# Seven 256-column products in place of four 512-column ones for the output projection of a state-space layer

## The chip, the core and the metric

The kernel runs on one core of a Trainium2 chip. A core has a matrix engine (TensorE, in the profile PE, with its weight loads as PEld), a vector engine (VectorE, DVE), a scalar engine (ScalarE, ACT), a general engine (GpSimd, POOL) and a queue engine (SyncE, SP) that issues most DMAs. Work is passed between them through SBUF and, for matmul results, through eight banks of PSUM. The metric is the device time of one launch in microseconds, over several runs.

## The reference

`reference()` computes a small model in float32 on x of 2 x 512 tokens x 512 features: a feed-forward layer, a state-space layer, the same feed-forward layer again, a memory layer, an attention layer, the memory layer again. The change is in the state-space layer (`_L0_attn_ref`): 128 heads of 64 channels make 8192 inner channels in 8 groups. The change touches what follows their gating:

```python
y = (Y_diag + Y_off).reshape(b, S, H_M, P_M)[:, :s] + D_res
y = y.reshape(b, s, D_INNER)
yg = y * jax.nn.silu(gate)
gsz = D_INNER // G_M
ygr = yg.reshape(b, s, G_M, gsz)
ygr = ygr * jax.lax.rsqrt(jnp.mean(ygr * ygr, axis=-1, keepdims=True) + EPS)
y = ygr.reshape(b, s, D_INNER) * gnorm_w
out = jnp.einsum('bsd,od->bso', y, out_proj_w)
return residual + out
```

Here b is 2, s 512, D_INNER 8192, G_M 8, and out has 512 columns. Because the norm is one factor per token and group, it can be applied after the product, group by group.

## The kernel before

The state-space layer is `ssm`. It goes through 128 steps, one for each of 64 tiles of 128 channels (`ct`) and each of two batches, in the order group g, batch b, tile q (eight tiles, so eight steps, for each group and batch; `PAIRS` is 8). `period(n)` writes out by hand the order of TensorE, VectorE, ScalarE and GpSimd for three steps in flight: `cur` (step n) is projected and convolved, `p1` (step n-1) has its state-space products, `p2` (step n-2) goes through the output projection. DMAs on SP aren't bound to that hand-written order; they are issued in the order that the scheduler of the framework chooses from it.

In a period TensorE goes through these lines:

- L1158, ht: four transposes of `p1.hid` (bank t). L1178 on VectorE multiplies them by dt into hc, L1187 on ScalarE by the decay into hd.
- L1128, called at many places: the seven products of two k-steps each that give hid and gate (already in Strassen's manner), into banks X, R and G, 256 columns at a time. ScalarE copies partial results between them (L1173 G, L1204 and L1242 u).
- L1213, st: states of `p1` from hd; VectorE chains them (L1223).
- L1078, po: the output projection, `gather`. For each of four chunks of 128 tokens one matmul: stationary a 128x128 piece of the gated result `yg`, moving the whole weight tile `wo` of 512 columns, summed into four banks `po` over the eight steps of a group. Chunks 0 and 1 come in the middle of the period, ahead of the last product into X ("ws3"), 2 and 3 at its end.
- L1268 and L1276, py: the state-space output of `p1`; VectorE adds the skip and multiplies with the gate (L1299, L1303 yg).

At the end of the period X is convolved: ScalarE L936 the first tap, VectorE L939 three more, ScalarE L1296 the silu, and the next period transposes it. `within` (L1047) and `times_c` (L1063) make the decay matrix M, ScalarE exponentiates it (L1055). GpSimd adds the squares of yg (L1123 ssum), makes Cs (L1068) from the broadcast `rows`, and in steps of batch 0 the sums of the next step's weights (L1024 to L1026, `add_up`), which `keep_sums` stores in DRAM for batch 1. In the sixth and seventh period of a group the next group's B and C are projected (L928), in the eighth their product (L986 cb) is made in bank t.

At a group's end `group_sums` and `group_norm` give the factor r, and `leave` (L1108) takes the four banks to x: four operations of 128x512, multiply and add, in the next period. The weight tile `wo` is loaded once for both batches (L348), scaled by `gnorm` on ScalarE (L1317) and kept in the pool `w2` of 12 tiles. After the 128 steps two more periods drain the pipeline, with the norm of the next feed-forward layer among them.

## Time and profile before

| | us |
|---|---|
| median of 3 runs | 2653.52 |
| lowest, highest | 2647.42, 2655.45 |
| the profiled execution | 2652.62 |
| its span, first to last instruction | 2650.9 |
| periods 1 to 127 of the state-space part (ht at 262.07 to ht at 2000.21) | 1738.1 |
| period 128 to the first matmul of the next layer (2018.92) | 18.7 |
| TensorE busy in L1078 (1024 passes) | 483.9 |

The page counts busy time per engine and follows one chain of waits back from the end. In its groups an f32 matmul appears as two records, one for each pass. The timeline merges neighbouring instructions of one line: start, time until the last of them ends, engine, line, operation, operands, shape, count, and in brackets how long the engine stood idle before and who released it. Matmuls overlap, so the step from one start to the next is what a group takes.

Period lengths repeat almost exactly from group to group: 13.31, 12.52, 12.52, 12.52, 15.96, 16.40, 13.60 and 12.55 us for the second to the eighth period of a group and the first of the next, the longer ones with L928, L986 and the group's sums. Periods 2 to 8, which also prepare decays for batch 1, take 105.8 us together.

### The profile page before, as it was taken

Reading aid. Unit: us, or ns where it says so; the run is one execution under the profiler, and the core shown is the slowest. Engines: PE = TensorE matmul, PEld = TensorE weight load, DVE = VectorE, ACT = ScalarE, POOL = GpSimd, SP = SyncE. Lnnn points to the kernel's source line nnn. Section 1 sums busy time; section 2 is a strip of 40 time slices with the busy share of each in tenths; the row PEclk is TensorE's granted clock in tenths of the full one; section 3 lists DMA queues with packets and bytes.
Section 4 is the critical chain, followed back from the end, with each engine's and each line's share of the span. In section 5 each row is a group of like instructions: output and inputs, shape, how many; then the busy total and the mean of one; then the engine's idle time right before and its main releaser. Section 6 shows DMA issues by size and latency. Waiting matters only on the chain.

```text
span 2650.9 us, 38083 instructions
## 1 busy us (share of the span) xinstructions
PE 2583.4 (97%) x13744; PEld 1685.5 (64%) x13744; DVE 1895.1 (71%) x4056; ACT 1587.9 (60%) x3247; POOL 597.0 (23%) x492
## 2 busy tenths in 40 slices
PE   8999999999999999999999999999998999899997
PEld 4445677777777777777777777777774444445453
DVE  7845987878778777777777878778786432666655
ACT  2214777777777677777777767777773211344433
POOL 0002322432332242242233234224320000111000
PEclk9999999999999999999999999999999999889988
DMA  6623444444444454444444444445441110000000
GB/s 204 197 78 116 175 151 168 181 150 189 156 175 167 153 192 153 166 171 175 175 159 165 179 162 171 171 153 192 152 175 42 40 59 24 1 1 2 1 1 32
DMA packets 90907, 342.93 MB, mean 129 GB/s; under 512 B 11520, under 2 KB 12096, under 8 KB 74208
## 3 DMA queue, kind: packets, MB, share of 16 engines
q1 hardware_dynamic: 87264, 330.86, 34.3%
q10 hardware_dynamic: 3168, 8.65, 0.8%
q8 instruction: 110, 1.80, 0.3%
q0 software_dynamic: 288, 0.98, 0.1%
q14 instruction: 77, 0.63, 0.1%
HBM read 295.10 MB, written 45.35 MB: 128 GB/s over the span
## 4 chain that ended last, share of the span: by engine, by line
PE 90%; DVE 6%; ACT 2%; issue 1%; POOL 0%; DMA 0%; SPq 0%; DVEq 0%; ACTq 0%; POOLq 0%
PE hid L1128 20%; PE po L1078 16%; PE gate L1128 9%; PE fmm L509 5%; PE fo L675 5%; PE py L1268 5%; PE st L1213 3%; PE py L1276 3%; PE fy L509 3%; PE cp_BT L928 2%; PE ht L1158 2%; PE cp_CT L928 2%; PE w L1806 1%; PE fdd L509 1%; PE pao L1866 1%; PE f L536 1%
## 5 line engine op out<-in xcount | busy, mean ns | idle before, releaser
L939 DVE SCALAR_TENSOR_TENSOR hid<-hid,small,hid 128x256 f32<-128x256 f32 (+3 forms) x768 | 368.7, 480 | 309.6 <-ACT hid L936 291.3
L1078 PE MATMUL po<-wo,yg 128*128 128x512 f32 x1024 | 483.9, 592 | 0.0
L1123 POOL TENSOR_TENSOR ssum<-ssum,sq 128x512 f32<-128x512 f32 x112 | 142.1, 1268 | 1048.8 <-ACT sq L1119 1048.8
L1047 DVE TENSOR_TENSOR_SCAN M<-rows,later 128x512 f32<-128x512 f32 x256 | 299.7, 1213 | 0.0
L1078 PEld LDWEIGHTS po<-wo,yg 128*128 128x128 f32 x1024 | 191.9, 190 | 127.7 <-issue 108.3
L1128 PE MATMUL hid<-mixed,wsum 128*128 128x256 f32 x1024 | 270.8, 387 | 0.3 <-ACT hid L1206 0.3
L1128 PE MATMUL hid<-hT_s,wgh 128*128 128x256 f32 x1024 | 264.7, 381 | 0.0
L1068 POOL TENSOR_TENSOR Cs<-CT,rows 128x768 f32<-128x768 f32 x128 | 233.4, 1823 | 2.0 <-PE hps_s L398 1.5
L1128 PEld LDWEIGHTS hid<-hT_s,wgh 128*128 128x128 f32 x1024 | 183.3, 190 | 23.0 <-ACT hid L1173 3.9
L1128 PEld LDWEIGHTS hid<-mixed,wsum 128*128 128x128 f32 x1024 | 184.0, 189 | 20.6 <-ACT hid L1206 0.7
L1187 ACT ACTIVATE hd<-ht,end 128x64 f32<-128x64 f32 x768 | 172.7, 330 | 9.1 <-DVE hc L1178 9.1
L1296 ACT ACT_TABLE_LOAD x128 | 164.2, 1283 | 2.3
L1063 DVE TENSOR_TENSOR M<-M,CB 128x512 f32<-128x512 f32 x256 | 164.4, 684 | 0.0
L1055 ACT ACT_TABLE_LOAD x127 | 162.9, 1283 | 2.2
L936 ACT ACTIVATE hid<-hid,small 128x256 f32<-128x256 f32 x256 | 143.6, 561 | 10.8 <-PE hid L1128 2.0
L1055 ACT ACTIVATE M<-M 128x512 f32<-128x512 f32 x256 | 147.8, 624 | 2.2 <-DVE M L1047 0.8
L1128 PE MATMUL gate<-mixed,wgh 128*128 128x256 f32 x512 | 141.6, 399 | 1.3 <-DVE v L1253 1.3
L1268 PE MATMUL py<-M,hc 128*64 128x128 f32 x2048 | 140.5, 280 | 0.0
L1128 PEld LDWEIGHTS hid<-hT_s,wsum 128*128 128x128 f32 x512 | 97.1, 190 | 67.9 <-issue 59.3
L1770 DVE CUSTOM_DVE_ANT_0 j<-s,future 128x384 f32<-128x384 f32 (+3 forms) x256 | 113.0, 487 | 37.2 <-PE s L1760 36.4
L1268 PEld LDWEIGHTS py<-M,hc 128*64 128x64 f32 x2048 | 109.6, 137 | 40.1 <-issue 37.7
L1128 PE MATMUL hid<-hT_s,wsum 128*128 128x256 f32 x512 | 131.5, 379 | 0.6 <-ACT u L1242 0.6
(341 smaller groups left out, 4606.0 us busy)
## 6 DMA issues: line engine op xcount, KB each, us to landing
rows<-rows SPq DMA_DIRECT2D x128, 1024.0 KB, 4.7
wgh<-in_w_gh_dram SPq DMA_DIRECT2D x128, 512.0 KB, 5.3
sums<-wsum SPq DMA_DIRECT2D x64, 512.0 KB, 3.0
wsum<-sums SPq DMA_DIRECT2D x64, 512.0 KB, 4.8
wo<-in_w_out_dram SPq DMA_DIRECT2D x64, 256.0 KB, 4.0
wbc<-in_w_bc_dram SPq DMA_DIRECT2D x16, 512.0 KB, 5.6
wi<-in_q_dram SPq DMA_DIRECT2D x44, 128.0 KB, 3.1
sc<-in_s_dram SPq DMA_DIRECT2D x44, 128.0 KB, 3.2
```

The costliest lines, as they stand in the source:

```text
L509: nc.tensor.matmul(dst, lhsT=w[:, k, :], rhs=x[:, k, :], start=start and k == 0, stop=stop and k == 1, skip_group_check=True,)
L936: self.nc.scalar.activation(out, p, AF.Identity, bias=w[:, 4:5], scale=w[:, 3:4])
L939: self.nc.vector.scalar_tensor_tensor(out=out, in0=p, scalar=self.convw[:, ct, 3 - s : 4 - s], in1=out, op0=ALU.mult, op1=ALU.add,)
L1047: self.nc.vector.tensor_tensor_scan(out=m, data0=cur.rows[:, i, 0, :], data1=self.later, initial=0.0, op0=ALU.add, op1=ALU.mult,)
L1055: self.nc.scalar.activation(m, m, AF.Exp)
L1063: self.nc.vector.tensor_tensor(out=m, in0=m, in1=sh["CB"], op=ALU.mult)
L1068: self.nc.gpsimd.tensor_tensor(out=cur.Cs, in0=sh["CT"][:, P:].unsqueeze(1).to_broadcast([P, 2, S - P]), in1=cur.rows[:, :, 1, P:], op=ALU ...
L1078: self.nc.tensor.matmul(self.po[c], lhsT=p2.yg[:, c * P : (c + 1) * P], rhs=self.wo[p2.ct], start=p2.q == 0, stop=p2.q == PAIRS - 1,)
L1128: self.nc.tensor.matmul(dst, lhsT=w[:, k, :], rhs=x[:, k, :], start=start and k == 0, stop=stop and k == 1, skip_group_check=True,)
L1187: nc.scalar.mul(hd[:, c, ch], pt[:, c, ch], self.dec["dt_end"][:, b1 * NC + c, h0 + i : h0 + i + 1],)
L1268: nc.tensor.matmul(py[ch, cs], lhsT=hc[:, c, ch], rhs=p1.M[i].rearrange("p (c t) -> p c t", c=NC)[:, c, :], start=c == 0, stop=c == 0, ski ...
L1296: nc.scalar.activation(cur.hid, cur.hid, AF.Silu)
```

## The change

- The output projection no longer runs step by step. The gated results `yg` of a group and batch are kept (eight tiles of two steps each, `pair_of`), and their projection runs during the next eight periods.
- For two neighbouring channel tiles, two chunks of tokens (h and 2+h) and the two halves of the output columns, the 2x2x2 block product is made with seven products instead of eight. A stage is one half h of a group and batch: seven products times four pairs of tiles, 28 matmuls of 256 moving columns, seven in each of four periods (`out_products`: four in the middle, one and two at the end). They go product by product, with three banks: OX, OR and OG; `out_seed` copies the first product from OX to OG.
- GpSimd makes the sums of yg that the products need (`out_sums`, 16 operations of 128x128 a stage).
- The weights are loaded two tiles at a time, scaled, their four differences made on GpSimd (`prepare`, `prepare_sums`), and all of it written to DRAM (`prepared`); each stage loads what it needs, 14 times 256 KB (`out_load`, a period ahead).
- `out_leave` adds a bank to a quarter of x: six operations of 128x256 a stage.
- hc, hd, st and the squares use buffers of other pools; `rows` is split in two loads, of which `starts` has one buffer and is read for Cs; `pr` has a bank of its own, and is no longer cleared by VectorE.
- `out_end` runs the last stages after the loop, with the first half of the next layer's norm between them; before, its statistics were in the last periods of the loop.

```diff
-            ctx.enter_context(self.banks("psum_s", t=1, po=4, X=1, G=1, R=1))
+            ctx.enter_context(self.banks("psum_s", t=1, OX=1, OG=1, OR=1, X=1, G=1, R=1, s=1))
             ctx.enter_context(self.in_order())
-            self.wo, self.done = {}, None
+            self.out_begin()
             self.load_rows(self.steps[0])
             for n in range(len(self.steps) + 2):
                 self.period(n)
+            self.out_end(len(self.steps) + 2)
...
     def load_rows(self, st):
-        st.rows = self.sp.tile([P, 2, 2, S], F32, tag="rows", name=f"rows{st.n}", bufs=2)
-        self.nc.sync.dma_start(
-            out=st.rows, in_=self.rows[st.b][st.h0 : st.h0 + 2].partition_broadcast(P)
-        )
+        rows = self.rows[st.b][st.h0 : st.h0 + 2].partition_broadcast(P)
+        st.rows = self.sp.tile([P, 2, S], F32, tag="rows", name=f"rows{st.n}", bufs=2)
+        self.nc.sync.dma_start(out=st.rows, in_=rows[:, :, 0])
+        st.starts = self.sp.tile([P, 2, S - P], F32, tag="starts", name=f"starts{st.n}", bufs=1)
+        self.nc.sync.dma_start(out=st.starts, in_=rows[:, :, 1, P:])
...
+    def out_begin(self):
+        self.pairs = [
+            self.sp.tile([P, 2, S], F32, tag=f"yg{i}", name=f"yg{i}", bufs=1)
+            for i in range(PAIRS // 2 + 1)
+        ]
+        self.A = {
+            x: self.sp.tile([P, PAIRS // 2, P], F32, tag=x, name=x, bufs=1)
+            for x in ("S1", "S2", "S34")
+        }
+        self.norms, self.banked, self.out_w, self.hold = {}, {}, {}, {}
+        self.made, self.raw = {}, None
+        half = lambda h: slice(h * HS, (h + 1) * HS)
+        low = lambda h: (0, slice(h * P, (h + 1) * P))
+        high = lambda h: (0, slice((2 + h) * P, (3 + h) * P))
+        odd = lambda f: lambda h: (1, f(h)[1])
+        self.order_out = [
+            ("OX", low, "raw", 0), ("OR", "S34", "sum", 2), ("OX", "S2", "sum", 1),
+            ("OG", odd(low), "raw", 2), ("OX", "S1", "sum", 0), ("OR", odd(high), "sum", 3),
+            ("OX", "S34", "raw", 3),
+        ]
...
+    def pair_of(self, i, k):
+        k = i % 2 * (PAIRS // 2) + k
+        if k <= PAIRS // 2:
+            return self.pairs[k]
+        name = "zeo"[k - PAIRS // 2 - 1]
+        if name not in self.hold:
+            self.hold[name] = self.early.tile([P, 2, S], F32, tag=name, name=f"yg_{name}")
+        return self.hold[name]
+    def prepare(self, n):
+        m, at = divmod(n, PAIRS)
+        g = (m + 1) // 2
+        if at % 2 == 0 or g == NG or m % 2 == 0 and m:
+            return
+        if at == 1:
+            self.made[g] = tuple(
+                self.dram.tile([PAIRS // 2, P, k, HS], F32, name=f"{x}{g}", tag=f"{x}{g}")
+                for x, k in (("oraw", 4), ("osum", 4))
+            )
+        ct = g * PAIRS + at - 1
+        self.raw = g, at // 2, [self.w2(self.a["w_out"][ct + k], f"wo{ct + k}") for k in range(2)]
+    def prepare_sums(self):
+        if self.raw is None:
+            return
+        g, i, raw = self.raw
+        for k in range(2):
+            ct = g * PAIRS + 2 * i + k
+            self.nc.scalar.mul(raw[k], raw[k], self.gnorm[:, ct : ct + 1])
+        made = [
+            self.w2pool.tile([P, 2, HS], F32, tag="w2", name=f"wos{g}_{i}_{k}") for k in range(2)
+        ]
+        (b11, b12), (b21, b22) = ((r[:, :HS], r[:, HS:]) for r in raw)
+        t1, t2, t3, t4 = (m[:, k] for m in made for k in range(2))
+        for out, in0, in1 in ((t1, b12, b11), (t2, b22, t1), (t3, b22, b12), (t4, b21, t2)):
+            self.nc.gpsimd.tensor_tensor(out=out, in0=in0, in1=in1, op=ALU.subtract)
+        self.raw += (made,)
+    def prepared(self):
+        if self.raw is None:
+            return
+        g, i, raw, made = self.raw
+        for dst, src in zip(self.made[g], (raw, made)):
+            for k in range(2):
+                self.nc.sync.dma_start(
+                    out=dst[i, :, 2 * k : 2 * k + 2],
+                    in_=src[k].rearrange("p (h d) -> p h d", h=2) if src is raw else src[k],
+                )
+        self.raw = None
...
+    def stage(self, n):
+        return divmod(n - PAIRS - 1, PAIRS // 2)
+    def out_load(self, n):
+        s, k = self.stage(n)
+        if not 0 <= s < 2 * NG * NB:
+            return
+        for one in range(7 * k, 7 * k + 7):
+            if one % 2 == 0:
+                bank, left, kind, part = self.order_out[one // 4]
+                raw, made = self.made[s // (2 * NB)]
+                ps = slice(one % 4, one % 4 + 2)
+                if kind == "raw":
+                    src = raw[ps, :, part]
+                else:
+                    src = made[ps, :, part]
+                t = self.w2pool.tile([P, 2, HS], F32, tag="w2", name=f"ow{s}_{one}")
+                self.nc.sync.dma_start(out=t, in_=src.rearrange("i p d -> p i d"))
+                self.out_w[s, one // 2] = t
+    def out_sums(self, n):
+        s, k = self.stage(n)
+        if not 0 <= s < 2 * NG * NB:
+            return
+        sub, add = ALU.subtract, ALU.add
+        h = s % 2
+        lo, hi = slice(h * P, (h + 1) * P), slice((2 + h) * P, (3 + h) * P)
+        for name, at, op in (
+            ("S3", 0, sub), ("S1", 0, add), ("S2", 1, sub), ("S4", 2, sub),
+        ):
+            if at != k:
+                continue
+            for i in range(PAIRS // 2):
+                y = self.pair_of(s // 2, i)
+                S1, S2, S34 = (self.A[x][:, i, :] for x in ("S1", "S2", "S34"))
+                out, in0, in1 = {
+                    "S3": (S34, y[:, 0, lo], y[:, 0, hi]),
+                    "S1": (S1, y[:, 0, hi], y[:, 1, hi]),
+                    "S2": (S2, S1, y[:, 0, lo]),
+                    "S4": (S34, y[:, 1, lo], S2),
+                }[name]
+                self.nc.gpsimd.tensor_tensor(out=out, in0=in0, in1=in1, op=op)
+    def out_products(self, n, a, b):
+        s, k = self.stage(n)
+        if not 0 <= s < 2 * NG * NB:
+            return
+        for one in range(7 * k + a, 7 * k + b):
+            j, i = divmod(one, 4)
+            bank, left, kind, part = self.order_out[j]
+            if i == 0 and j < 2:
+                self.banked[bank, s] = self.ps(bank, [P, S], f"{bank}{s}")[:, :HS]
+            if isinstance(left, str):
+                l = self.A[left][:, i, :]
+            else:
+                q, cs = left(s % 2)
+                l = self.pair_of(s // 2, i)[:, q, cs]
             self.nc.tensor.matmul(
-                self.po[c], lhsT=p2.yg[:, c * P : (c + 1) * P], rhs=self.wo[p2.ct],
-                start=p2.q == 0, stop=p2.q == PAIRS - 1,
+                self.banked[bank, s], lhsT=l, rhs=self.out_w[s, one // 2][:, one % 2, :],
+                start=one in (0, 4), stop=one in (15, 23, 27), skip_group_check=True,
+            )
+    def out_seed(self, n):
+        s, k = self.stage(n)
+        if k == 0 and 0 <= s < 2 * NG * NB:
+            g = self.banked["OG", s] = self.ps("OG", [P, S], f"OG{s}")[:, :HS]
+            self.nc.scalar.copy(g, self.banked["OX", s])
...
+    def out_leave(self, n, spot):
+        s, k = self.stage(n)
+        for at, where, bank, row, col, back in (
+            (0, 0, "OR", 1, 0, 1), (0, 0, "OX", 0, 1, 1), (1, 1, "OR", 1, 1, 0),
+            (2, 0, "OX", 1, 0, 0), (2, 1, "OG", 0, 0, 0), (3, 0, "OX", 1, 1, 0),
+        ):
...
+        self.prepared()
+        self.out_load(n + 1)
+        if cur is not None:
+            self.prepare(n)
+            if nxt is not None:
+                self.load_rows(nxt)
+        self.out_sums(n)
...
+            hc, hd, st = (
+                self.held(self.npool, "h", x, 3).rearrange("p (c k) -> p c k", c=NC)
+                for x in ("hc", "hd", "st")
+            )
...
+        self.out_leave(n, 0)
+        if p1 is not None:
...
-        if p2 is not None:
-            self.gather(p2, 0, 1)
+        self.out_products(n, 0, 4)
...
-            p1.yg = sp.tile([P, S], F32, tag="yg", name=f"yg{p1.n}", bufs=2)
+            p1.yg = self.pair_of(NB * p1.g + p1.b, p1.q // 2)[:, p1.q % 2, :]
...
-        if p1 is not None and p1.b == 0:
-            wt = self.w2(a["w_out"][p1.ct], f"wo{p1.ct}")
-            nc.scalar.mul(wt, wt, self.gnorm[:, p1.ct : p1.ct + 1])
-            self.wo[p1.ct] = wt
+        self.prepare_sums()
...
-            self.gather(p2, 2)
+        self.out_products(n, 4, 5)
         if after is not None and q == PAIRS - 1:
             self.group_cb(*after, "t")
-        if p2 is not None:
-            self.gather(p2, 3)
+        self.out_products(n, 5, 7)
...
+    def out_end(self, n):
+        hT, steps, turn = self.normed = self.ffn_norm(1)
+        stats, root, over, centre = steps
+        for i in range(PAIRS):
+            self.out_load(n + i + 1)
+            self.out_sums(n + i)
+            self.out_leave(n + i, 0)
+            self.out_products(n + i, 0, 4)
+            self.out_seed(n + i)
+            self.out_leave(n + i, 1)
+            self.out_products(n + i, 4, 7)
+            if i == 0:
+                for t in range(NC):
+                    stats(t)
+                root(0, NC)
+                over(0, NC)
+            elif i <= NC:
+                centre(i - 1)
+                turn(i - 1, "XG"[i % 2])
...
-    nc = bacc.Bacc("TRN2", target_bir_lowering=False, num_devices=1)
+    nc = bacc.Bacc(
+        "TRN2", target_bir_lowering=False, num_devices=1, dynamic_dma_scratch_size=8192
+    )
```

## The prediction

> **What bounds the kernel now.** I read the page's busy shares and chain first, then the TensorE timeline of one ordinary period of the state-space part, then the other engines in that period, then the period that has no out-product.
>
> ```profile
> PE 2583.4 (97%) x13744; PEld 1685.5 (64%) x13744; DVE 1895.1 (71%) x4056; ACT 1587.9 (60%) x3247; POOL 597.0 (23%) x492
> PE 90%; DVE 6%; ACT 2%; issue 1%; POOL 0%; DMA 0%; SPq 0%; DVEq 0%; ACTq 0%; POOLq 0%
> 379.24:1986.87 1607.63, 1607.42 (x9232) 1179.70 (x9230) 1262.28 (x2436) 1197.42 (x2515) 499.49 (x404) 1.00 0.45 169
> ```
>
> TensorE sets the end: 90% of the chain, and in the stretch of periods 9 to 126 (third line: PE, PEld, DVE, ACT, POOL, clock, DMA share, GB/s) it rests 0.2 us in 1608, at full clock. So a column taken off TensorE there is time gained until another engine's chain is longer. The matmuls of one ordinary period (12.53 us from ht to ht):
>
> ```profile
> 405.07 0.60 PE L1158 MATMUL ht<-masks,hid 128*128 128x128 f32 x4
> 405.51 1.03 PE L1128 MATMUL hid<-hT_s,wgh 128*128 128x256 f32 x4
> 406.38 1.03 PE L1128 MATMUL gate<-mixed,wsum 128*128 128x256 f32 x4
> ...
> 410.56 1.88 PE L1078 MATMUL po<-wo,yg 128*128 128x512 f32 x4
> 412.28 1.03 PE L1128 MATMUL hid<-hT_s,wsum 128*128 128x256 f32 x4
> ...
> 415.88 1.88 PE L1078 MATMUL po<-wo,yg 128*128 128x512 f32 x4
> 417.60 0.60 PE L1158 MATMUL ht<-masks,hid 128*128 128x128 f32 x4
> ```
>
> Read starts, not durations (these overlap). Each f32 matmul is two passes. Four 512-wide passes take 410.56 to 412.28 = 1.72 us, 0.43 each; four 256-wide ones 405.51 to 406.38 = 0.87, 0.215 each. Half the columns cost half the time, with no fixed price. The out-product (gather) has 8 passes a period, 3.44 us.
>
> **The main term.** Seven 256-wide products replace four 512-wide ones: 14 passes x 0.215 = 3.01 us, 0.43 less a period. A 256-wide pass must hide a weight load of 190 ns (the PEld rows), and does so in L1128 already. More waits (a streamed weight for every second product, sums from POOL) need semaphores; the 51 ns semaphore events in front of L1128's and L1268's groups run ahead of the array and leave the 0.215 unchanged, so I take nothing for them; the upper bound is 51 ns for each of 3.5 loads, 0.18 us a period.
>
> A page of the Trainium skill speaks against this: "TensorE: Matmul & The Clock Gate", section "Back-to-back issue gap", puts sustained spacing at 81 ns for 128 columns and 131 ns for 512, so narrow matmuls pay much more per column. Interpolated, my estimate is 98 ns at 256, and 14 of these against 8 of 131 would make the out-product 1.31 times dearer, about 1.1 us a period lost and a time near 2790. The rows above (0.215 against 0.43) do not agree with it for this f32 stream, and they decide.
>
> Periods 9 to 127 all carry products before and after: 119 x 0.43 = **-51.2 us**.
>
> **What the shorter period uncovers.** TensorE is shorter by 0.43 only at the end of a period (gather 2 and 3 were 1.72, three products are 1.29; the middle stays 1.72). The covered chain is ws3 product, first tap, taps, silu, ht; and on DVE yg, v, M, hc, then hd on ACT, then st:
>
> ```profile
> 414.26 1.52 DVE L939 SCALAR_TENSOR_TENSOR hid<-hid,small,hid 128x256 f32<-128x256 f32 x3 [2.43 <-ACT hid L936]
> 415.82 0.63 ACT L1296 ACTIVATE hid<-hid 128x512 f32<-128x512 f32 x1 [0.29 <-DVE hid L939]
> 417.42 1.28 DVE L1063 TENSOR_TENSOR M<-M,CB 128x512 f32<-128x512 f32 x2
> 418.62 0.69 DVE L1178 TENSOR_TENSOR hc<-ht,dt 128x512 f32<-128x512 f32 x1
> 419.37 1.35 ACT L1187 ACTIVATE hd<-ht,end 128x64 f32<-128x64 f32 x6
> 421.49 0.72 PE L1213 MATMUL st<-hd,Btok 128*128 128x128 f32 x5
> ```
>
> silu ends 416.45, ht starts 417.60: slack 1.15. hd ends 420.72, st starts 421.49: slack 0.77. Both outlast 0.43. Two kinds of period do not. In the eighth of a group the cb matmuls already start as yg lets go of their bank, and ht waits for CB: nothing is gained there, 14 x 0.43 = **+6.0**. In the second period of a group silu's slack at the next ht is only 0.63 (the norm's ACT work); 0.20 is left, and out_seed puts an ACT copy (0.37, as L1242's) ahead of the taps: with a semaphore some 0.24 x 15 = **+3.6**. FFN's stats leave the last four periods, where they made st wait: **-1.1** (13.34, 12.68 and 12.66 against 12.52).
>
> **Work that I cost at nothing in these periods, and its cover.**
> - DVE: six leaves of 128x256 in four periods. The taps of that shape take 0.48, so 2.9 us against 1.5 (four of 743 ns in eight periods). Cover: DVE's 2.43 idle before the late taps. They are put behind hc, so st is not late; the worst period has two, 0.97, leaving 2.43 - 0.43 - 0.97 = 1.0. Without cover, +0.36 a period.
> - POOL: L1025's 128x256 takes 756 ns and L1024's 128x512 1313, so 128x128 some 0.48: 16 sums, 7.7 us in four periods, 3.8 in the first. POOL sits 10.15 idle before ssum (410.71), so ssum, Cs and add_up behind them are on time. prepare_sums' four (3.0 us) come late in odd periods of b=1, where add_up (2.8) is absent. DVE's operations lasted the same beside POOL as without it (484 ns both).
> - ACT: 2 multiplies of 0.71 before silu(v), where ACT waits 1.08 for v, 0.93 more before L1173; before, it was one every b=0 period.
> - SP: some five issues more of 0.32. rows lose the wait on Cs; starts, with one buffer, has it, and keep_sums, fetch, prepared and out_load queue behind it. That is mid-period; products need their load over a period later, and a load lands in 4.0 us (wo).
> - DMA, per b=1 period in engine time, with the mean packet of the trace (8 KB 349 ns, 4 KB 175, 2 KB 100, 1 KB 55): rows 128 x 349, now 512 of 1.5 to 2 KB, the same 45 us; weights and sums 45; out weights 3.5 x 256 x 55 = 49; raw load and two writes 38. 177 / 16 = 11.1 us of a 13.2 us period: 84%, where the window shows 45%. It fits. 1 KB packets are few (256), so bounds: 46 ns (their median) and 100 (never dearer than a 2 KB one); by the latter 13.6 us, over the period by 0.4.
>
> **Periods 2 to 8** carried a gather and now carry none, so the products are still owed at the end. Period 1 shows such a period:
>
> ```profile
> 262.07 0.63 PE L1158 MATMUL ht<-masks,hid 128*128 128x128 f32 x4 [1.25 <-ACT M L1055]
> 268.54 1.10 PE L1128 MATMUL hid<-hT_s,wsum 128*128 128x256 f32 x4 [0.61 <-ACT u L1242]
> 273.42 0.66 PE L1158 MATMUL ht<-masks,hid 128*128 128x128 f32 x4 [1.04 <-ACT hid L1296]
> ```
>
> 11.35 us, not 12.52 - 3.44: TensorE waits for u and silu. So of 3.44 only some 1.2 comes back in periods 2 to 4, and 2 to 3 in 5 to 8 (conv, decay and cb matmuls give cover): **-13** of 24.1. Bounds 0 and -24.1.
>
> **The end.** From period 128's ht (2000.21) to FFN's first matmul (2018.92) it is 18.7 now. After: period 128, 8.8 to its last product; period 129, 7.5: its first product waits for two leaves (0.97 and latency, 1.4), group_sums waits for ssum behind eight POOL sums (3.8), seven products and pr; out_end's seven product stages 7 x 3.01 = 21.1, plus 1.8 where a product waits for a leave queued behind four stats (0.87 each) and the root, 0.8 at the second stage start, and four turns of 0.44: 25.5. Together 41.8, **+23**. Bounds: +15 if products fill what was idle (5.8), +30.
>
> **Sum**: -51.2 + 6.0 + 3.6 - 1.1 - 13 + 23 = -32.7. From the profiled execution's 2652.6 (span 2650.9, 1.7 around it; 0.9 below the median of 2653.52): **2620**.
>
> **Rivals.**
> 1. *All slack holds, early periods shrink fully, the end costs 15*: -51 - 24 - 1 + 15 = -61, 2592. For it: the even slacks. Against it: period 1.
> 2. *Part is eaten*: semaphores at their bound of 0.18 a period take 21, or the early periods and tail fall at their dear ends: 2640 to 2660. For it: the hd slack falls to 0.34. Against it: 53 ns spacing of L1268's matmuls shows that issue has room.
> 3. *DVE's and ACT's chain becomes the bound* (slower): ws3, taps, M, hc, hd, st. It decides once that chain is 0.34 later a period, and wipes out the gain of the loop at 0.77: then -13 + 23 = +10, 2663. Against it: leaves lie behind hc.
> 4. *The streamed weights become the bound* (slower): DMA engines, b=1 periods. It begins at (16 x 13.2 - 128) / 896 = 93 ns a 1 KB packet and eats the gain at 0.6 us a period more, 104 ns. At 126 ns (the slow tail of the 1 KB packets, their 95th percentile) 15.1 us a period, 1.8 x 56 = 100: 2720. For it: 84% by means. Against it: TensorE waits for no DMA now, and 55 ns is well below.
> 5. *It does not do what it says*: had 256-wide passes a fixed price, seven for eight would give nothing; the pitch rows exclude it.
>
> **How the numbers follow.** Forecast 0.56 (2605 to 2640), bigger gain 0.10, part eaten 0.14, chain 0.07, DMA 0.13. 0.3% (8 us) is about what can be told from no change: below 2645.5 are the first two and a fifth of the third: faster 0.69; within, the rest of the third: 0.11; slower 0.20. The range leaves out most of the DMA case and the lowest of the bigger gain: 2598 to 2662.
>
> **What would show it.** Right: product passes at 0.215 pitch, ordinary periods of 12.1 us, PE rest in the loop under 10 us, periods 2 to 8 near 93 us (105.8 now), some 42 from period 128's ht to FFN. Wrong: product passes waiting for DMA or POOL, DMA share over 90% in b=1, ordinary periods still at 12.5, ht or st waiting in each.

## The result, and the profile after

| | before | after |
|---|---|---|
| median of the paired runs, us | 2650.47 | 2684.57 |
| lowest, highest | 2644.93, 2655.45 | 2682.97, 2687.63 |
| ratio, 95% interval | | 1.0131 [1.0105, 1.0156] |
| span of the profiled execution | 2650.9 | 2681.2 |
| start to period 2 | 273.4 | 273.9 |
| periods 2 to 8 | 105.8 | 105.5 |
| periods 9 to 127 ("the loop" below) | 1621.0 | 1628.9 |
| period 128's ht to FFN's first matmul ("the tail") | 18.7 | 42.2 |
| the rest | 631.9 | 630.7 |

The change made the kernel slower by 1.3%. The forecast was 2620, faster. The table, made from the starts of the ht groups, already says where it failed. The tail grew by 23.5 us, as foretold. The loop should have lost 42.7 us and gained 7.9. Periods 2 to 8 should have lost 13 and lost 0.3.

The page after: busy shares, the chain of waits, and two of the costliest groups (count, then busy us and mean ns of one, then idle time ahead of it and who ended it):

```profile
PE 2569.1 (96%) x14512; PEld 1819.9 (68%) x14512; DVE 1966.8 (73%) x4168; ACT 1583.1 (59%) x3279; POOL 1024.4 (38%) x1132
PE 59%; DVE 26%; ACT 11%; issue 2%; POOL 1%; DMA 1%; ACTq 0%; SPq 0%; POOLq 0%; DVEq 0%
...
L1345 ACT ACTIVATE held_hd<-ht,end 128x64 f32<-128x64 f32 x768 | 171.2, 322 | 56.2 <-DVE held_hc L1337 56.0
...
L1065 DVE TENSOR_TENSOR M<-M,CB 128x512 f32<-128x512 f32 x256 | 190.6, 785 | 0.0
```

TensorE is busy 14 us less than before, but the chain runs through it for 59% only, where it was 90%; VectorE has 26%. ScalarE's hd waits 56 us for hc (9.1 before), and one product M x CB takes 785 ns instead of 684 though it is the same instruction on the same shapes. The loop's window (columns as in the prediction) and TensorE's waits in the loop (total, number, longest):

```profile
379.10:2008.34 1629.24, 1601.46 (x10018) 1310.49 (x10019) 1336.61 (x2557) 1202.66 (x2567) 896.32 (x992) 1.00 0.73 243
```

```profile
PE ht L1314 <- ACT hid L1452: 11.6, 16, 0.8
PE st L1371 <- ACT held_hd L1345: 8.8, 29, 0.7
PE hid L1279 <- ACT hid L1329: 3.9, 14, 0.3
PE hid L1279 <- ACT hid L1401: 1.9, 12, 0.2
```

TensorE rests 27.8 us at full clock, and no line names a DMA or GpSimd: all four name ScalarE. These totals are too small. TensorE's timeline of the period after one in which GpSimd made the weights' differences shows why:

```profile
1300.00 1.03 PE L1279 MATMUL hid<-hT_s,wgh 128*128 128x256 f32 x4
1300.87 1.03 PE L1279 MATMUL hid<-mixed,wsum 128*128 128x256 f32 x4
1302.24 0.94 PE L1371 MATMUL st<-held_hd,Btok 128*128 128x128 f32 x6 [0.34 <-ACT held_hd L1345]
1303.01 1.08 PE L1279 MATMUL hid<-mixed,wsum 128*128 128x256 f32 x4
1303.93 1.46 PE L1218 MATMUL OR<-ow,yg 128*128 128x256 f32 x6
1305.22 0.59 PE L1218 MATMUL OX<-ow,S 128*128 128x256 f32 x2
```

Four passes should need 0.87 (1300.00 to 1300.87). The next four are followed by st only after 1.37, so st is 0.50 late; the bracket says 0.34, since the last pass is drawn beyond the point at which the next could have started. I therefore add up lateness from start to start (every step of the loop that is over 0.11 us longer than its columns need; py is left out). "G product" is the product into bank G that follows ScalarE's copy L1329, ws3 the last product into X, pr the small matmul of a group's sums:

| late, us in the loop | all | st | ht | G product | ws3 | cb, OX, pr |
|---|---|---|---|---|---|---|
| before | 3.2 | 0.7 | 2.5 | 0 | 0 | 0 |
| after | 47.0 | 14.2 | 16.9 | 6.3 | 6.0 | 3.6 |

Smaller delays are not counted: without the lateness in this table after's loop would be 1581.9, and that of c1 (below, 1587.2 with 13.2 late) 1574.0, so some 8 us more of after's loop are delays under 0.11.

The last two lines of the fence show what was right: six product passes in 1303.93 to 1305.22 are 0.215 each, with streamed weights and sums from GpSimd. The price of the main term was right; what it uncovered was not.

What makes these late shows in the second period of a group (period 81, ht at 1369.18). The timeline of all engines, thinned:

```profile
1368.97 0.92 POOL L1201 TENSOR_TENSOR S<-yg_z 128x128 f32<-128x128 f32 x1
...
1369.83 1.54 DVE L1065 TENSOR_TENSOR M<-M,CB 128x512 f32<-128x512 f32 x2
1369.86 0.97 POOL L1201 TENSOR_TENSOR S<-yg_e 128x128 f32<-128x128 f32 x1
...
1371.29 0.68 DVE L1337 TENSOR_TENSOR held_hc<-ht,dt 128x512 f32<-128x512 f32 x1
...
1371.89 0.47 DVE L1243 SCALAR_TENSOR_TENSOR x<-OR,r,x 128x256 f32<-128x256 f32 x1
...
1372.01 1.34 ACT L1345 ACTIVATE held_hd<-ht,end 128x64 f32<-128x64 f32 x6 [0.97 <-DVE held_hc L1337]
...
1372.29 0.47 DVE L1243 SCALAR_TENSOR_TENSOR x<-OX,r,x 128x256 f32<-128x256 f32 x1
...
1372.68 2.66 DVE L1049 TENSOR_TENSOR_SCAN M<-rows,later 128x512 f32<-128x512 f32 x2
...
1375.26 1.48 DVE L940 SCALAR_TENSOR_TENSOR hid<-hid,small,hid 128x255 f32<-128x255 f32 x3
...
1376.83 0.15 ACT L1401 COPY hid<-hid 128x3 f32<-128x3 f32 x1 [1.18 <-DVE hid L940]
...
1383.77 0.66 PE L1314 MATMUL ht<-masks,hid 128*128 128x128 f32 x4 [0.73 <-ACT hid L1452]
```

Two M x CB take 1.54 (1.28 before) with GpSimd's sums S beside them, and the sums take 0.92 and 0.97 where they take 0.46 alone. The two scans take 2.66 (2.33 before). So hc, hd and st are late. Then two leaves lie between hc and the scans, and the taps behind the scans release a copy of three columns on ScalarE (L1401), for which ScalarE stands 1.18; everything behind it on ScalarE (exponentials, seed, first tap, root, silu) is late at the next ht. The leaves do lie behind hc, as the prediction said; it did not ask what lies behind the leaves.

Sorting VectorE's operations in the loop by whether GpSimd ran meanwhile:

| after, mean ns (largest) | no overlap | over 90% overlapped |
|---|---|---|
| M x CB, both inputs in SBUF | 682 (686) | 898 (1220) |
| scan, both inputs in SBUF | 1203 (1216) | 1389 (1690) |
| multiply into yg, both inputs in SBUF | 692 (693) | 759 (886) |
| late taps, one input in PSUM | 484 (487) | 484 (486) |
| hc, one input in PSUM | 681 (685) | 678 (683) |

In the kernel before, none of the M x CB and scans of the loop overlaps GpSimd at all: at the start of its period 81 add_up ends at 1362.72, and the M x CB start at 1363.56:

```profile
1361.99 0.73 POOL L1026 TENSOR_TENSOR wsum<-wsum,wgh 128x256 f32<-128x256 f32 x1
...
1363.56 1.28 DVE L1063 TENSOR_TENSOR M<-M,CB 128x512 f32<-128x512 f32 x2
...
1365.36 2.33 DVE L1047 TENSOR_TENSOR_SCAN M<-rows,later 128x512 f32<-128x512 f32 x2
```

### The profile page after: what moved, and what is told of

Its sections match the earlier page's. It is cut to its first block, busy times and chain, and to the rows that moved or that the text cites. A ratio compares the mean times of both kernels' runs of the same rounds, so it can differ in the third digit from the quotient of the medians.

```text
span 2681.2 us, 41940 instructions
## 1 busy us (share of the span) xinstructions
PE 2569.1 (96%) x14512; PEld 1819.9 (68%) x14512; DVE 1966.8 (73%) x4168; ACT 1583.1 (59%) x3279; POOL 1024.4 (38%) x1132
## 4 chain that ended last, share of the span: by engine, by line
PE 59%; DVE 26%; ACT 11%; issue 2%; POOL 1%; DMA 1%; ACTq 0%; SPq 0%; POOLq 0%; DVEq 0%
PE hid L1279 11%; DVE hid L940 5%; PE fmm L509 5%; PE fo L675 5%; DVE M L1049 5%; PE gate L1279 4%; PE OX L1218 4%; DVE M L1065 4%; ACT L1057 3%; PE fy L509 3%; PE py L1424 2%; PE st L1371 2%; ACT M L1057 2%; PE cp_CT L929 2%; PE py L1432 1%
## 5 line engine op out<-in xcount | busy, mean ns | idle before, releaser
L1274 POOL TENSOR_TENSOR held_ssum<-held_ssum,held_sq 128x512 f32<-128x512 f32 x112 | 142.3, 1271 | 559.1 <-ACT held_sq L1270 545.7
L1049 DVE TENSOR_TENSOR_SCAN M<-rows,later 128x512 f32<-128x512 f32 x256 | 315.2, 1271 | 0.0
L1070 POOL TENSOR_TENSOR Cs<-CT,starts 128x768 f32<-128x768 f32 x128 | 234.1, 1829 | 3.4 <-DMA starts<-rows 3.4
L1345 ACT ACTIVATE held_hd<-ht,end 128x64 f32<-128x64 f32 x768 | 171.2, 322 | 56.2 <-DVE held_hc L1337 56.0
L1218 PE MATMUL OX<-ow,S 128*128 128x256 f32 x768 | 199.4, 380 | 1.3 <-DVE x L1243 1.2
L1065 DVE TENSOR_TENSOR M<-M,CB 128x512 f32<-128x512 f32 x256 | 190.6, 785 | 0.0
L1218 PEld LDWEIGHTS OX<-ow,S 128*128 128x128 f32 x768 | 142.2, 190 | 23.4 <-POOL S L1201 2.9
L1424 PE MATMUL py<-M,held_hc 128*64 128x128 f32 x2048 | 140.1, 279 | 0.0
L1424 PEld LDWEIGHTS py<-M,held_hc 128*64 128x64 f32 x2048 | 109.2, 136 | 39.0 <-issue 37.3
L1279 PE MATMUL gate<-mixed,wsum 128*128 128x256 f32 x512 | 133.5, 384 | 0.0
```

The lines of the kernel that those rows point to most:

```text
L1049: self.nc.vector.tensor_tensor_scan(out=m, data0=cur.rows[:, i, :], data1=self.later, initial=0.0, op0=ALU.add, op1=ALU.mult,)
L1065: self.nc.vector.tensor_tensor(out=m, in0=m, in1=sh["CB"], op=ALU.mult)
L1070: self.nc.gpsimd.tensor_tensor(out=cur.Cs, in0=sh["CT"][:, P:].unsqueeze(1).to_broadcast([P, 2, S - P]), in1=cur.starts, op=ALU.mult,)
L1218: self.nc.tensor.matmul(self.banked[bank, s], lhsT=l, rhs=self.out_w[s, one // 2][:, one % 2, :], start=one in (0, 4), stop=one in (15, 23 ...
L1279: self.nc.tensor.matmul(dst, lhsT=w[:, k, :], rhs=x[:, k, :], start=start and k == 0, stop=stop and k == 1, skip_group_check=True,)
L1345: nc.scalar.mul(hd[:, c, ch], pt[:, c, ch], self.dec["dt_end"][:, b1 * NC + c, h0 + i : h0 + i + 1],)
```

## The experiments

The places of lateness are as above; loop, periods 2 to 8 and tail come from the profiled execution, M x CB and scan are means over 400 to 1900 us. Ratios are to the kernel before, run again beside each group of experiments (medians 2647.9 to 2652.5).

| run | median | ratio, 95% interval | loop | 2 to 8 | tail | M x CB, scan ns |
|---|---|---|---|---|---|---|
| after | 2684.57 | 1.0131 [1.0105, 1.0156] | 1628.9 | 105.5 | 42.2 | 793, 1268 |
| e1 | 2661.52 | 1.0038 [1.0020, 1.0057] | 1608.0 | 104.2 | 39.5 | 735, 1234 |
| e2 | 2677.97 | 1.0109 [1.0084, 1.0135] | 1622.0 | 106.1 | 41.4 | 802, 1271 |
| e3 | 2668.20 | 1.0074 [1.0049, 1.0099] | 1617.4 | 105.5 | 43.6 | 738, 1239 |
| e5 | 2686.65 | 1.0139 [1.0118, 1.0161] | 1629.6 | 106.5 | 42.4 | 795, 1269 |
| c1 | 2641.21 | 0.9960 [0.9944, 0.9975] | 1587.2 | 105.4 | 40.9 | 684, 1208 |
| d1 | 2652.84 | 1.0005 [0.9990, 1.0019] | 1621.4 | 104.4 | 18.8 | 739, 1221 |
| d2 | 2651.36 | 0.9994 [0.9982, 1.0007] | 1621.4 | 104.2 | 21.6 | 684, 1208 |
| p1 | 2681.49 | 1.0114 [1.0091, 1.0138] | 1629.4 | 106.1 | 40.8 | 793, 1270 |
| s1 | 2671.61 | 1.0078 [1.0060, 1.0095] | 1618.7 | 105.0 | 43.5 | 792, 1269 |
| v2 | 2661.36 | 1.0043 [1.0027, 1.0059] | 1612.2 | 105.7 | 42.4 | 735, 1207 |
| v1 | 2636.91 | 0.9940 [0.9925, 0.9956] | 1586.3 | 105.2 | 43.9 | 750, 1222 |
| v3 | 2638.56 | 0.9962 [0.9949, 0.9975] | 1586.9 | 102.9 | 40.8 | 783, 1225 |

| late in the loop, us | all | st | ht | G product | ws3 | cb, OX, pr |
|---|---|---|---|---|---|---|
| after | 47.0 | 14.2 | 16.9 | 6.3 | 6.0 | 3.6 |
| e1 | 29.8 | 6.8 | 14.2 | 6.2 | 0 | 2.6 |
| e2 | 41.9 | 14.2 | 16.0 | 8.0 | 0 | 3.6 |
| e3 | 37.7 | 5.6 | 17.0 | 6.7 | 6.0 | 2.4 |
| c1 | 13.2 | 0.5 | 2.8 | 7.4 | 0 | 2.5 |
| s1 | 40.8 | 14.2 | 16.9 | 0 | 6.0 | 3.6 |
| v2 | 32.9 | 3.4 | 10.1 | 12.0 | 0 | 7.4 |
| v1 | 13.0 | 4.7 | 3.4 | 0 | 0 | 4.9 |

**e1: GpSimd's sums of yg in the first stage only.**

```diff
     def out_sums(self, n):
         s, k = self.stage(n)
-        if not 0 <= s < 2 * NG * NB:
+        if s != 0:
             return
```

> Leaves out the 16 GpSimd sums of all stages but the first (the products use the first stage's sums, so the state-space result is another). Collision theory (GpSimd's added work slows VectorE's operations that read two SBUF inputs, M times CB and the scan, and hc, hd and st come late): M times CB in the first periods of a stage back to 0.68 us, st waits in the second and sixth period of a group gone, ws3 waits smaller, 15 to 25 us less than the changed kernel (2660 to 2670). Order theory (two leaves ahead of the scan and the first taps hold ScalarE's copy into X): waits of ws3 (0.3) and of ht (0.9) in the second period of a group stay, at most 5 us less. DMA theory (the streamed weights set the pace): no change.

The loop lost 20.9 us, st's lateness halved and ws3's went; ht's fell only from 16.9 to 14.2, so the sums are not the main thing that makes silu late.

**e2: the leave of OR in the second place of its period.**

```diff
-            (0, 0, "OR", 1, 0, 1), (0, 0, "OX", 0, 1, 1), (1, 1, "OR", 1, 1, 0),
+            (0, 1, "OR", 1, 0, 1), (0, 0, "OX", 0, 1, 1), (1, 1, "OR", 1, 1, 0),
```

> Moves the leave of bank OR in a stage's first period from ahead of the scan to VectorE's idle time ahead of the late taps. Order theory: ScalarE's copy into X comes 0.47 earlier in the second and sixth period of a group, ws3's wait of 0.3 there gone, ht's wait in the second period 0.3 to 0.4 shorter: 6 to 10 us less (about 2676). Collision theory and DMA theory: within 3 us of the changed kernel.

6.9 us of the loop, with M x CB as slow as in after: the place of one 0.47 us leave is worth that much by itself. It takes away ws3's 6.0. The second period gets 0.41 shorter, as expected, but the lateness of ht falls by 0.9 in all.

**e3: weights prepared for the first group only** (every stage then uses those).

```diff
-        if at % 2 == 0 or g == NG or m % 2 == 0 and m:
+        if at % 2 == 0 or g:
             return
...
-                raw, made = self.made[s // (2 * NB)]
+                raw, made = self.made[0]
```

> Prepares the weights of the first group alone and uses them for all groups (another result): seven eighths of the raw loads, ScalarE multiplies, GpSimd differences and DRAM writes are gone. Collision theory: the slow M times CB after the second, fourth, sixth and eighth period of every other group goes, st waits of 0.56 there with it: 5 to 10 us less. Order theory: no change. DMA theory: some 45 MB fewer, about as much less as in the run with half the stream.

11.5 us of the loop, a little over the 5 to 10 expected; 8.6 of the lateness that went is st's (14.2 to 5.6). This takes away ScalarE's scaling and the stores too, so it does not yet say that it is GpSimd.

**e5: every second of the streamed weight loads left out**, its products using the load ahead of it.

```diff
             if one % 2 == 0:
+                if one % 4:
+                    self.out_w[s, one // 2] = self.out_w[s, one // 2 - 1]
+                    continue
```

> Loads every second streamed weight tile alone and uses it twice (another result): 224 loads and 57 MB fewer, all else the same. Collision and order theory: within 4 us of the changed kernel. DMA theory: a third or more of what was lost comes back, 20 us or more.

The loop did not move: 1629.6 against 1628.9. The streamed loads do not set its pace.

**c1: e1, e2, e3 together, and no copy from OX to OG.**

```diff
-                start=one in (0, 4), stop=one in (15, 23, 27), skip_group_check=True,
+                start=one in (0, 4, 12), stop=one in (15, 23, 27), skip_group_check=True,
...
-            self.nc.scalar.copy(g, self.banked["OX", s])
```

> Leaves out GpSimd's sums of yg after the first stage, the weights' scaling, differences and stores after the first group, and ScalarE's copy from OX to OG (OG then starts at its own product); the leave of OR is in the second of its places. All that was blamed, at once. Theory (collisions, order of the leaves, ScalarE's added work account for the whole loss of the loop): single removals took 20.9, 11.5 and 6.9 us off the loop; with the copy gone some 3 more, so loop 1583 to 1592 against 1628.9, M times CB near 690 ns, scan near 1210, the tail still 39 to 42 and periods 2 to 8 still 104 to 106; median 2636 to 2644. Rival (the shorter period itself uncovers a chain that none of these touches, so the 0.43 cannot be had): loop stays above 1600, median above 2652.

1587.2, inside what the theory gave. M x CB is back at 684 ns and the scan at 1208. The page of c1:

```profile
PE 86%; DVE 8%; ACT 4%; issue 1%; POOL 0%; DMA 0%; SPq 0%; ACTq 0%; DVEq 0%; POOLq 0%
...
L1065 DVE TENSOR_TENSOR M<-M,CB 128x512 f32<-128x512 f32 x256 | 165.9, 690 | 0.0
```

So the 0.43 a period is there to be had, with the slacks of 0.34 and 0.7 that the prediction worked out; what remains is the product into G (7.4).

**d1: the kernel before, with GpSimd's 16 subtractions in each four periods added**, on constants, at the place of the sums.

```diff
+            self.dump = self.sp.tile([P, P], F32, tag="dump", name="dump", bufs=1)
...
+        for _ in range((8, 4, 4, 0)[(n - 9) % 4] if n > 8 else 0):
+            nc.gpsimd.tensor_tensor(
+                out=self.dump, in0=self.ident, in1=self.ident, op=ALU.subtract
+            )
```

> The kernel before, unchanged but for GpSimd: 16 subtractions of 128x128 in each four periods, on constants, at the place where the change makes its sums; nobody waits for them. Theory (two-input SBUF operations of VectorE and GpSimd disturb each other, whatever they belong to): M times CB 684 to 740-800 ns, scan 1208 to 1230-1270, operations with a PSUM operand unchanged, and the loop longer by 2 to 12 us only, since hd has 0.77 us of slack there. Rival, the prediction's (no disturbance): all durations and the loop unchanged within 2 us. Rival (the slowing in after is contention with its 284 thousand DMA packets, not with GpSimd): durations unchanged here.

GpSimd's and VectorE's timelines where the eight subtractions meet the two M x CB, which took 1.28 before:

```profile
1359.54 6.60 POOL L1156 TENSOR_TENSOR dump<-masks 128x128 f32<-128x128 f32 x8
```

```profile
1360.40 1.49 DVE L1064 TENSOR_TENSOR M<-M,CB 128x512 f32<-128x512 f32 x2
1361.81 0.68 DVE L1183 TENSOR_TENSOR hc<-ht,dt 128x512 f32<-128x512 f32 x1
1362.41 2.57 DVE L1048 TENSOR_TENSOR_SCAN M<-rows,later 128x512 f32<-128x512 f32 x2
```

The disturbance belongs to the two engines and not to the change: overlapped M x CB take 885 ns, hc is as ever, and d1 adds no transfer. The mean durations moved to 739 and 1221, just below the ranges given. The loop did not move: 1621.4 against 1621.0, where the theory gave 2 to 12 us more. This GpSimd work costs nothing where st has 0.77 us of slack; taking it away gave 20.9 us where st has 0.34 and the change's other work stands beside it.

**d2: the kernel before without the output products of periods 2 to 8.**

```diff
+        if p2.g == p2.b == 0 and p2.q < PAIRS - 1:
+            return
         for c in chunks:
...
-                start=p2.q == 0, stop=p2.q == PAIRS - 1,
+                start=p2.q == 0 or p2.g == p2.b == 0, stop=p2.q == PAIRS - 1,
```

> The kernel before without the products into po of periods 2 to 8 (the first seven tiles of the first group and batch are left out of the sum). Measures the gain that the prediction counted for these periods with none of the change's other work. The prediction's step: 105.8 goes to about 93, the median 13 us down. Theory now (the chain of ScalarE and VectorE with the set-up work sets these periods, TensorE's products only filled its waits): 101 to 105, median within 5 us of before. Rival (the change's own weight preparation ate the gain): 93 here and clearly less than in after.

104.2 against 105.8. The 24.1 us of products there were nearly free: without them TensorE waits instead. Its longest waits for hid between 273 and 382 us in before, in d2 and in after:

```profile
PE ht L1158 <- ACT hid L1296: 1.9, 3, 1.0
```

```profile
PE ht L1160 <- ACT hid L1298: 9.1, 5, 2.9
PE hid L1130 <- ACT hid L1246: 5.1, 7, 0.8
```

```profile
PE ht L1314 <- ACT hid L1452: 8.6, 5, 2.9
PE hid L1279 <- ACT hid L1401: 4.8, 6, 1.2
```

The same two waits in d2 and after, of nearly the same length: silu of hid, and ScalarE's copy ahead of ws3.

A second thing took from the gain: with less to do, TensorE's granted clock fell in this stretch. The windows of before, d2 and after (the clock is the third number from the end):

```profile
273.00:380.00 107.00, 102.90 (x565) 72.70 (x566) 93.42 (x158) 77.93 (x161) 37.90 (x29) 0.98 0.42 154
273.00:380.00 107.00, 86.06 (x515) 64.74 (x516) 92.95 (x158) 78.38 (x163) 38.03 (x29) 0.95 0.42 151
273.00:380.00 107.00, 85.19 (x508) 64.02 (x509) 93.29 (x155) 77.33 (x161) 57.79 (x52) 0.95 0.62 204
```

In the clock's record the halved stretches of periods 2 to 8 sum to 3.4 us in before, 10.2 in d2 and after, and none in d1, where the same work as before's took 104.4. If all of it lay on TensorE's path, 10.2 us at half clock cost 5.1 us, so at full clock d2 would have taken at least 99.1: at most 5.3 less than d1's 104.4, out of 24.1, and not 13.

**p1: the first group's weights neither scaled nor differenced.**

```diff
     def prepare_sums(self):
...
         g, i, raw = self.raw
+        if g == 0:
+            self.raw += ([r.rearrange("p (h d) -> p h d", h=2) for r in raw],)
+            return
```

> The changed kernel with the first group's weights neither scaled nor differenced (the raw tiles are stored in both places; all transfers stay). If the preparation on ScalarE and GpSimd is what keeps periods 2 to 8 at 105.5: they fall to 93 to 98, and the median by 8 to 12. If the chain with the set-up work binds without it: 103 to 105, median within 3 us of the changed kernel. Loop and tail unchanged by both.

106.1, above the 103 to 105 of the second case and with 13.7 us at half clock: the preparation is not what holds these periods.

**s1: the silu of the next group's B and C moved** behind the next period's first tap.

```diff
+        if n > 0:
+            for one in self.owed:
+                one[2]()
         if n < 2:
             nc.scalar.copy(X[:, 1:4], G[:, 1 + HS : 4 + HS])
...
-        for one in late:
-            one[2]()
+        self.owed = late
```

> All of the reference is computed. The changed kernel with one thing moved: the silu of the next group's B and C goes from the end of its period to behind the next period's first tap, so ScalarE's copy of G does not lie behind it. Theory (the shorter period took ScalarE's last slack in front of that copy): the wait of 0.44 in n%8=6 and 0.11 in n%8=7 goes, loop 6 to 9 us shorter than 1628.9, median 2676 to 2680. Rival (the copy waits for something else): no change in these periods, loop within 2 us.

The lateness of the product into G goes from 6.3 to 0, all other places unchanged, and the loop is 10.2 us shorter: more than expected, because the eighth period also fell, from 13.66 to 13.45 (the seventh from 16.42 to 15.89).

**v2: only GpSimd's work moved, nothing left out.** A one-column copy of the scan's result makes GpSimd wait for the scan; the sums follow, S1 behind add_up; the weights' differences come a period later, behind Cs.

```diff
+            s, k = self.stage(n)
+            if s >= 0 and k < 3:
+                mark = sp.tile([P, 1], F32, tag="mark", name=f"mark{n}", bufs=1)
+                nc.gpsimd.tensor_copy(mark, cur.M[1][:, S - 1 :])
+            self.out_sums(n, 0)
             self.first_tap(cur.hid[:, :HS], G[:, V], ct)
...
                 if nxt is not None:
                     self.add_up(nxt)
+            self.prepare_made()
+            self.out_sums(n, 1)
```

> All of the reference is computed. Only GpSimd's work is moved (sums of yg behind the scan, S1 behind add_up, the weights' differences behind Cs in even periods); nothing is left out and nothing else moved. Theory (when GpSimd's work lies matters, not that it is there): M times CB near 690 to 720 ns, scan near 1215, loop 1600 to 1608 against 1628.9 (without the sums alone it was 1608.0, without the later weights 1617.4), median 2656 to 2666. Rival (the amount of GpSimd's work decides, through queues or DMA): loop above 1620.

1612.2, 4 us above what the theory allowed and well below the rival: 16.7 us of the loop for moving the same work. The scan is back at 1207 ns; M x CB is at 735, not under 720. The wait for the G copy grew from 6.3 to 12.0, so part of the gain was lost there; in v1, where the silu is moved too, it is 0.

**v1: v2, s1 and e2 together**, the copy to OG early in the next period (ahead of its products), and all seven products of period 128 ahead of st.

```diff
     def out_seed(self, n):
         s, k = self.stage(n)
-        if k == 0 and 0 <= s < 2 * NG * NB:
+        if k == 1 and 0 <= s < 2 * NG * NB:
...
+        if cur is None:
+            self.out_products(n, 0, 7 if p1 is not None else 4)
         if p1 is not None:
             pst = self.ps("t", [P, NC, P], f"st{p1.n}")
```

> All of the reference is computed. The parts blamed, moved instead of left out: GpSimd's sums of yg start behind the scan (a one-column copy of the scan's result makes GpSimd wait for it), S1 behind add_up; the weights' differences behind Cs in the even periods of batch 1; the leave of OR and the copy to OG in later places; the silu of the next group's B and C behind the next period's first tap; in period 128 all seven products ahead of st. Theory: loop 1583 to 1597 (c1 without these parts had 1587, the silu's move is worth 7, what still overlaps costs some), tail 37 to 40, periods 2 to 8 as they were, median 2632 to 2648: faster than before by 0.1 to 0.8%. Rival (GpSimd's work cannot be placed free of VectorE's two-input operations, or the waits that place it cost as much): loop over 1605, median above 2655.

2636.91, a ratio of 0.994 [0.9925, 0.9956] to before: faster than both kernels. TensorE's waits in its loop, and one batch-0 period on GpSimd and VectorE:

```profile
PE st L1392 <- ACT held_hd L1355: 1.6, 7, 0.2
PE pr L1262 <- POOL held_ssum L1282: 1.3, 7, 0.2
PE ht L1324 <- ACT hid L1474: 0.8, 1, 0.8
```

```profile
1343.16 1.06 POOL L1150 TENSOR_TENSOR wos<-wo,wos 128x256 f32<-128x256 f32 x1
...
1348.30 0.19 POOL L1374 COPY mark<-M 128x1 f32<-128x1 f32 x1 [2.26 <-DVE M L1049]
1348.43 0.46 POOL L1209 TENSOR_TENSOR S<-yg 128x128 f32<-128x128 f32 x1
```

```profile
1342.74 2.02 DVE L1065 TENSOR_TENSOR M<-M,CB 128x512 f32<-128x512 f32 x2
...
1348.15 1.49 DVE L940 SCALAR_TENSOR_TENSOR hid<-hid,small,hid 128x255 f32<-128x255 f32 x3
```

The mark waits 2.26 for the scan, and then the sums take 0.46 each beside taps that keep their 1.49. Of what is left, the fence shows the last weights of a group (wos, 1.06), which spill into the next batch-0 block and stretch M x CB to 2.02; in all, 49 of the loop's M x CB are still slowed, 14 beside such differences and 35 beside add_up and S1's sums. The tail was to fall to 37 to 40 and did not (43.9): the wait for hd in period 128 (3.4) went, but the waits for leaves ahead of OX grew from 2.3 to 3.4, the states cost a new 1.3, and TensorE's clock was halved for 6.8 us of it (last section).

**v3: v1 with the weights prepared one period earlier.**

```diff
-        if at % 2 == 0 or g == NG or m % 2 == 0 and m:
+        odd = int(m == 0)
+        if at % 2 != odd or g == NG or m % 2 == 0 and m:
...
```

> All of the reference is computed. As v1_all_valid, but the weights of the next group are prepared one period earlier, so the last pair's differences do not fall into the first period of a batch-0 block, where add_up already fills GpSimd and pushes them into M times CB and the scan (wos 1.06 to 1.21 us each there, M times CB 2.02 us for its two). Theory (when GpSimd's work lies matters): the waits of st (0.39) and pr (0.35) in the second period of those blocks shrink, that period goes from 13.85 towards 12.93 in 7 groups, loop 1579 to 1583 against 1586.3, median 2629 to 2635. Rival (these waits come from add_up and S1 alone): period stays at 13.85, loop within 1 us.

Half a hit: the second period of batch-0 blocks fell from 13.85 to 13.33, but the fifth of the other blocks rose from 12.11 to 12.44, where the differences, now made in the same period as S4's sums, run over into the next M x CB, and the loop stayed at 1586.9. Time taken off one place on a full GpSimd came back at another.

## Why the prediction was wrong, step by step

**The main term was right.** Passes take 0.215 with no cost of semaphores or streamed loads, and six of the eight ordinary periods of two blocks take 12.11 to 12.27 in after; the two with the weights' differences beside them take 12.44 and 12.75, and 12.17 and 12.11 in e3. The loops of c1 and v1 are 33.8 and 34.7 us shorter than before's, with 13 us of lateness still in each.

**"DVE's operations lasted the same beside POOL as without it (484 ns both)": the step that failed most.** The row was the late taps, which read PSUM. M x CB on the path to st, and the scan on the path to the first taps, have both inputs in SBUF and never overlapped GpSimd in the loop of before, so that trace could not answer the question and I let a neighbouring row answer it. Measured: 682 to 898 ns and 1203 to 1389 when overlapped. Leaving the sums out gave 20.9 us (e1), moving all of GpSimd's new work gave 16.7 (v2), and d1 shows that the disturbance needs nothing else of the change.
A page of the Trainium skill has this rule, and I passed over it. "SBUF — State Buffer", section "Who interferes with whom", says that a VectorE instruction with two SBUF inputs contends with a GpSimd instruction that reads SBUF, and one with at most one SBUF input does not; section "SBUF: two separate sides" adds that the winner keeps the shared ports for its whole instruction. The table above agrees in every row. Taken literally, an M x CB behind one whole sum lasts 682 + 455 = 1137 ns, my estimate from the two durations; the largest measured beside sums was 947. The 1220 stood beside a weights' difference (0.73 alone), where the same estimate gives 1412. So the trace shows who contends; these two waits of VectorE, 265 and 538 ns, are shorter than the whole neighbour.

**"They are put behind hc, so st is not late" (the leaves).** True of st; but behind the leaves on VectorE lie the scans and the first taps, then ScalarE's copy, then ws3 and the exponentials. The 2.43 us of idle that I named as cover comes later in the period than this chain. Price 6.9 us (e2).

**"2 multiplies of 0.71 before silu(v), where ACT waits 1.08 for v, 0.93 more before L1173".** Those were gaps of ordinary periods. In the seventh and eighth period of a group the silu of B or C fills the place in front of that copy, and ScalarE had no gap there. Price 10.2 us (s1). The multiplies were not what cost it: c1 has none of them in its loop and still 7.4 us there. The shorter period uncovered this copy, and the prediction's list of periods without slack had the second and the eighth, but not the seventh.

**"some 0.24 x 15 = +3.6", the second period.** It was to take 13.31 - 0.43 + 0.24 = 13.12 and took 14.60 and 14.18; silu's lateness at ht is the largest item of the table (16.9). Three things meet there: the slow M x CB and scans (e1 takes 0.60 off this period), the leave (e2, 0.41), and the copy to OG, which no run takes away alone. By difference, an estimate: in blocks of batch 1, v2 has 13.59, the leave is worth 0.41, and v1 has 12.90, so 0.28 are left for the copy (s1 left this period as it was), near the 0.24 foretold. The copy's size was about right; the other two were missing from the term.

**Periods 2 to 8, -13 of 24.1.** They gave 0.3 in after and 1.6 in d2. I read period 1, found 1.2 of 3.44 to come back in such a period, and added more for later periods because conv, decay and cb matmuls would give cover. Next to nothing came back: the products had filled waits for ScalarE, and without them the clock was halved for 10.2 us instead of 3.4. This is a term of the right sign, eight times too large by d2 and more by after.

**Right**: the eighth period in after (no gain; cb and ht 0.17 late each; but s1 gained 0.21 there, so the silu was half of it), the end (+23 foretold, +23.5 measured, with 3.4 us at half clock in it), and that the DMA engines do not bind (no wait of TensorE in the loop names one, e5 unchanged). Their share was put too high: 84% in batch-1 periods, where it measured 71%, and 73% over the loop.

**The rivals.** What happened is the third, the chain of VectorE and ScalarE, which I gave 0.07. I put the point from which it decides at 0.34 us a period for st, and c1, where st is late by only 0.5 us in the loop with that slack, agrees with it. Its price, 2663, was 20 us too low: it was taken with the 13 us of the early periods still in hand (12.7 of them did not come), and the loop did not only lose its gain but became 7.9 us longer than before's.

**The sum.** Of 63 us between forecast and profiled execution, 50.6 are in the loop and 12.7 in periods 2 to 8. Of the 50.6, moving work (v1) recovered 42.6: GpSimd's place, the leave, the silu and the copy to OG; v2, e2 and s1 alone sum to 33.8, and how the copy and their interplay share the rest was not separated. Between v1's loop and the forecast's 1578.3 there are 8.0 left; v1 still shows 7.2 us of lateness in st and pr.

## What to carry to other kernels

A slack is worth something only to the operation that ends it: before calling work on another engine free, list for the chain that ends the slack where each operation's inputs lie, and look in the trace for the same operation beside the same neighbour; if it never overlapped, the trace has no answer and the bound is open. An operation that is put "behind" something is ahead of something else, and that list is part of its price. Work taken from an engine in a stretch where it waits for others gave next to nothing back (here 1.6 of 24.1), and work added to a stretch with idle time is free only up to the slack left after the change (here 0.77 against 0.34).

## What the runs showed of the hardware

VectorE's operations with two inputs in SBUF and GpSimd's slow each other in both directions. M x CB went from 682 ns to 898 and the scan from 1203 to 1389. Beside them a 128x128 sum on GpSimd, 0.455 us alone, took up to 1.384, and a 128x256 difference, 0.73 alone, up to 1.703; taps that read PSUM stayed at 484 ns throughout.

In the early periods and the tail TensorE's granted clock fell after it had rested. Windows of after around the 2.87 us wait for silu in the early periods (columns as above, the clock is the third from the end):

```profile
284.00:287.90 3.90, 1.03 (x7) 0.81 (x7) 3.79 (x9) 3.61 (x5) 1.37 (x2) 1.00 0.91 293
287.90:291.40 3.50, 3.50 (x11) 2.76 (x10) 3.35 (x4) 1.62 (x7) 0.00 (x0) 0.52 0.87 300
291.50:295.00 3.50, 2.96 (x17) 2.35 (x15) 2.29 (x8) 2.20 (x6) 0.56 (x1) 1.00 0.44 152
```

After 3.9 us with 1.03 of work the clock is 0.52 for 3.5 us, then full again. The Trainium skill, "TensorE: Matmul & The Clock Gate", section "Part 1: The HAM clock gate (the "warmup" mystery)", gives activity windows of 3413 ns, after an idle one of which the clock is halved; the length agrees with these traces, though the stretch before it still held 1.03 us of matmuls. So a wait of this length can cost more than itself. In the state-space part such stretches, of 3.4 or 6.8 us, came in some runs and not in others: v1's tail, with one of 6.8, took 43.9, and v3's, the same code with the same waits at full clock, 40.8.
